# Feed-forward norms reach the features' partitions by block transposes and a way through DRAM instead of TensorE transposes

## The chip, the cores and the metric

The kernel runs on one core of a Trainium2 chip. The metric is the device time of one execution in microseconds (us). The engines are TensorE (PE in the profile; PEld is its weight load), VectorE (DVE), ScalarE (ACT), GpSimd (POOL) and SyncE (SP), which here only issues DMAs. All data is float32.

## The reference, cut to what matters

```python
# x: 4 sequences x 512 tokens x 256 features
n = layernorm(x)                                  # no gain, no bias
q = silu(n @ Wq1 @ Wq2);  f = sigmoid(n @ Wk1 @ Wk2);  v = n @ Wv
a = sigmoid(f)                                    # exp(log_sigmoid(f))
h = scan over tokens: h = a * h + (1 - a) * v
o = q * h;  o = o * rsqrt(mean(o * o) + 1e-6) * norm_w
x = x + layernorm(o @ Wo)

y = layernorm(x)
for i in range(6):
    y = gelu(y @ W1[i].T + B1[i]) @ W2[i].T + B2[i] + y     # 256 -> 1024 -> 256
    if i < 5:
        y = layernorm(y) * LN_G[i] + LN_B[i]
out = x + layernorm(y)
```

## The kernel before, in words

A tile holds 128 partitions. Matrix products want features on the partitions: an activation of one sequence is two tiles `xt` (128 features x 512 tokens). A norm wants tokens on the partitions, since its mean and variance run over the features: `sm` and `n` hold 128 tokens x 256 features. Going from one layout to the other is a transpose, done on TensorE by `transpose` (L504) into a PSUM tile and copied out by ScalarE (`to_features`).

The attention part runs first, over the 4 sequences. Then the feed-forward part runs over blocks i = 0 to 5 and, in each, over two groups g of two sequences (1024 tokens). For each (i, g):

- `Hidden` computes the first layer in 26 steps. Each step is two products of 256 columns (`product`, L493). The 4 x 2 by 2 x 4 blocks of the product are formed with fewer multiplications, from sums of weight blocks (`sa`, by `w1_sums`) and of blocks of the input (`tx`, by `input_sums`), both made by GpSimd (L459). The steps are in the text RESULT: the first is `a21 b10`, the second `s1 t1`, with t1 = b13 - b12. VectorE and ScalarE combine the products into the hidden blocks, and ScalarE applies the gelu (`Row.got`).
- `Row.got` also forms four sums t1 to t4 for the second layer, when all blocks of a row are there: t1 and t3 on VectorE (from `b12`, which lies in a PSUM bank), t2 and t4 on GpSimd. The blocks of row 0 come last, with the 26th step.
- `Output` computes the second layer with 28 products of 512 columns, four in each of the parts p1, p2, p6, p5, p7, p4, p3. The parts p4 and p3 are put off into the next `Hidden`. `partial` and `total` add bias and residual.
- `Norm` does the layer norm of that output while the next `Hidden` runs: `tokens` transposes it on TensorE (four 128x128 transposes per call, four calls), copies to `sm`, and takes statistics on VectorE; `rstd_of` gets the reciprocal deviation on GpSimd; `norm` normalizes on ScalarE into `n`; `features` transposes `n` back on TensorE (four transposes per call, four calls), and an activation applies gain and bias into `xt`. After the fourth, `input_sums` follows. In the last block there is no `features`: `norm` adds the attention's result x and stores. `Attended` has the same interface for the norm in front of block 0 (`ffn_input` also uses `to_features`).

The order of the work is not that of the source alone. `plan.op` records every operation with an engine, a cost, its reads and writes. `Plan.latest` gives each a due time, counted back from TensorE's sequence in the source; `Plan.run` simulates the engines with the costs, and at each moment lets an engine take the ready operation that is due first. The operations are issued in that order; every engine, and SP's queue of DMAs, then works in order on the chip. So a cost in the plan changes the order, not the operation. For DMAs the plan counts 0.3 us, the bytes, and 2.2 us.

Buffers are handed out by `Ring` (in turn) or `Pool` (taken and given back). `load` (L514) and `store` (L524) issue DMAs on SP: the inputs at the start, the 1 MB of `w1` and of `w2` for each block, and the outputs.

Of the kernel before, what the change touches and what calls it, by code (L numbers as in the profile page):

```python
# [16 lines left out]
P = 128  # L17
LN_EPS = 1e-5
SIGN = {"+": ALU.add, "-": ALU.subtract}
RMS_EPS = 1e-6  # L20
WARM = 6
# [52 lines left out]
p1 = s1 t1  # L74
# [95 lines left out]
class Ring:  # L170
# [5 lines left out]
    def next(self):  # L176
        buf = self.bufs[self.n % len(self.bufs)]
        self.n += 1
        if isinstance(buf, Grid):
            return buf.taken()  # L180
        buf.turn += 1
        return buf[:]


class Pool:


    def __init__(self, bufs):
        self.free = list(bufs)

    def next(self):
        buf = self.free.pop(0)
        buf.turn += 1
        return buf[:]

    def back(self, *views):
        self.free += [b for v in views for b in v.bufs]


class Grid:  # L200
# [9 lines left out]
    def taken(self):  # L210
        for b in sum(self.bufs, []):
            b.turn += 1
        lease = copy.copy(self)
        lease.views = {
            (m, k): self.view(m, k) for m in (None, 0, 1) for k in (None, 0, 1)
        }
        return lease
# [13 lines left out]
    def part(self, m=None, k=None):  # L231
        return self.views[m, k]


class Plan:
# [23 lines left out]
    def lag(self, before, after):  # L259

        a, b = self.ops[before], self.ops[after]
        if a[0] == b[0]:
            return 0.0
        return 0.35 if a[0] == "PE" else 0.2
# [64 lines left out]
def kernel(  # L329
# [41 lines left out]
    ps = ctx.enter_context(tc.tile_pool(name="ps", bufs=1, space=PSUM))  # L371
    ctx.enter_context(tc.manual_schedule())
# [12 lines left out]
    xs = [tiles(f"x{b}", [P, E], NT) for b in range(B)]  # L385
# [37 lines left out]
    hts = Ring([Grid(b.ap) for b in tiles("ht", [P, 2, S], NH)])  # L423
    tcs = Ring(tiles("tc", [P, S], 3 * NP))
    sms = Ring(tiles("sm", [P, 2, E], 4))
    nns = Ring(tiles("n", [P, E], 12))
# [8 lines left out]
    def act(dst, src, func=AF.Copy, bias=None, scale=None):  # L435
        given = [(k, p) for k, p in (("bias", bias), ("scale", scale)) if p is not None]
        ptrs = [p for _, p in given if isinstance(p, View)]
        kw = {k: p.ap if isinstance(p, View) else p for k, p in given}
        plan.op(
            "ACT",  # L440
            0.15 + 0.00083 * src.size + 0.11 * len(ptrs),
            lambda: nc.scalar.activation(dst.ap, src.ap, func, **kw)  # L442
            if func != AF.Copy
            else nc.scalar.copy(dst.ap, src.ap),  # L444
            [src, *ptrs],
            [dst],
        )
# [4 lines left out]
    def tt(engine, dst, a, b, alu):  # L452
        cost = 0.2 + 0.00209 * dst.size if engine == "POOL" else 0.06 + 0.00122 * dst.size
        if alu == ALU.pow:
            cost = 0.3 + 0.18 * dst.size
        plan.op(
            engine,
            cost,
            lambda: on(engine).tensor_tensor(dst.ap, a.ap, b.ap, alu),  # L459
            [a, b],  # L460
            [dst],
        )

    def tscalar(engine, dst, src, s0, s1, op0, op1=None):
        by = [s.ap if isinstance(s, View) else s for s in (s0, s1)]
        kw = {} if op1 is None else {"op1": op1}
        cost = (0.2 if engine == "POOL" else 0.15) + 0.0013 * dst.size
        if engine == "POOL":
            cost += 0.0017 * dst.size
        plan.op(  # L470
            engine,
            cost,
            lambda: on(engine).tensor_scalar(dst.ap, src.ap, *by, op0, **kw),  # L473
            [src, *(s for s in (s0, s1) if isinstance(s, View))],
            [dst],
        )

    def stt(dst, a, scalar, b, op0, op1):
        by = scalar.ap if isinstance(scalar, View) else scalar
        plan.op(  # L480
            "DVE",
            0.06 + 0.00133 * dst.size,
            lambda: nc.vector.scalar_tensor_tensor(dst.ap, a.ap, by, b.ap, op0, op1),  # L483
            [a, b, *([scalar] if isinstance(scalar, View) else [])],
            [dst],
        )
# [22 lines left out]
    def load(dst, src, engine="SP"):  # L509
        queue = nc.sync if engine == "SP" else nc.scalar  # L510
        plan.op(
            engine,
            0.45,
            lambda: queue.dma_start(out=dst.ap, in_=src),  # L514
            [],
            [dst],
            dst.size * P * 4 / 0.26e6,
        )

    def store(dst, src):  # L520
        plan.op(
            "SP",
            0.45,
            lambda: nc.sync.dma_start(out=dst, in_=src.ap),  # L524
            [src],
            [],
            src.size * P * 4 / 0.26e6,
        )
# [93 lines left out]
    def token_stats(mv, src, t):  # L622

        st = sts.next()

        def emit():
            nc.vector.bn_stats(st.ap, src.ap)  # L627
            nc.vector.bn_aggr(mv.ap[:, t, :], st.ap)  # L628

        plan.op("DVE", 0.59, emit, [src], [st, mv])  # L630
# [29 lines left out]
    def to_features(srcs, d, xt, scale=None, bias=None):  # L660
# [5 lines left out]
        if scale is None:  # L666
            act(xt, pt)
        else:
            act(xt, pt, AF.Identity, bias, scale)

    class Attention:
# [55 lines left out]
        def k1_q1(self):  # L727
            self.k1 = self.inner(wk1_s)
            self.q1 = self.inner(wq1_s)
            self.o, self.sq = [], []  # L730

        def value(self, e):
            self.psv = self.projected([wv_s[:, d, ts(e, P)] for d in range(ND)])

        def scan(self, e):
# [16 lines left out]
                1.3,  # L752
# [7 lines left out]
            o, sq = both.part(0), both.part(1)  # L760
            tt("POOL", o, q, h, ALU.mult)
# [23 lines left out]
        def residual(self):  # L785
# [4 lines left out]
            for t in range(NT):  # L790
                product(pss[:, t : t + 1], self.sq[-1][:, ts(t, P)], ones, True)
            ve = rs.next()[:, 0, :]
# [11 lines left out]
            for t in range(NT):  # L804
# [3 lines left out]
                token_stats(mv1, x1, t)  # L808
            self.x1_by = rstd_of(mv1, rs.next())
# [8 lines left out]
    class Row:  # L818
# [18 lines left out]
        def got(self, c, negative):  # L837
# [4 lines left out]
            if len(there) < 2:  # L842
                return
            if n == 1:
                self.b12 = banks.next()
# [11 lines left out]
            if len(self.there[1 - n]) == 2:  # L857
# [3 lines left out]
                tt("DVE", t1, self.b12, b11, ALU.subtract)  # L861
                tt("DVE", t3, b22, self.b12, ALU.subtract)
                banks.back(self.b12)
# [55 lines left out]
    class Output:  # L919


        def __init__(self, i, g, hidden):
# [5 lines left out]
            self.x = xts[g]  # L928
            self.a11 = [w[:, 2 * j, :P] for j in range(NP)]
            self.a12 = [w[:, 2 * j + 1, :P] for j in range(NP)]  # L930
            self.a22 = [w[:, 2 * j + 1, P:] for j in range(NP)]
            self.sf = [[None] * 2 for _ in range(ND)]
# [9 lines left out]

        def p1(self, j):
            if j == 0:
                self.px = banks.next()
            product(self.px, self.a11[j], self.hidden.rows[j].h[0][0], j == 0)
            if j == NP - 1:
                self.sn1 = self.partial(0, 0)

        def p2(self, j):  # L950
            if j == 0:
                self.py = banks.next()
            product(self.py, self.a12[j], self.hidden.rows[j].h[1][0], j == 0)
            if j == NP - 1:
# [3 lines left out]
        def p6(self, j):  # L958
            product(self.px, sb2[1][:, j, :], self.hidden.rows[j].sums[1], False)
            if j == NP - 1:  # L960
                self.sn2 = self.partial(0, 1)

        def p5(self, j):
            if j == 0:
                self.pz = [banks.next()[:, cols] for cols in self.parts]
            for pz, cols in zip(self.pz, self.parts):
                t1 = self.hidden.rows[j].sums[0]
                product(pz, sb2[0][:, j, :], t1[:, cols], j == 0)

        def p7(self, j):  # L970
            product(self.px, sb2[2][:, j, :], self.hidden.rows[j].sums[2], False)
            if j == NP - 1:
                self.s11 = self.partial(1, 1)
                if len(self.parts) == 1:
                    self.total11()

        def total11(self):
# [5 lines left out]
        def p4(self, j):  # L983
            product(self.px, self.a22[j], self.hidden.rows[j].sums[3], False)
            if j == NP - 1:
# [4 lines left out]
        def p3(self, j, part=0):  # L990
            pz, cols = self.pz[part], self.parts[part]
            b22 = self.hidden.rows[j].h[1][1]
            product(pz, sb2[3][:, j, :], b22[:, cols], False)
            if j == NP - 1:
# [9 lines left out]
    class Norm:  # L1004


        def __init__(self, i, g, output):
            self.i, self.g, self.output = i, g, output
            self.sm, self.by, self.n = [], [], []
# [25 lines left out]
        def norm(self, u):  # L1035

            for t in (2 * u, 2 * u + 1):
                z = normalized(self.sm[u][:, t % 2, :], self.by[t // NT], t % NT)
                self.n.append(z)
                if self.i == NB - 1:  # L1040
                    b, c = 2 * self.g + t // NT, t % NT
                    tt("POOL", z, z, xs[b][c], ALU.add)
                    store(out[b, ts(c, P), :], z)

# [14 lines left out]
        def features(self, u):  # L1059
            if self.i == NB - 1:  # L1060
                return
            n, d = divmod(u, ND)
            to_features(
                self.n[n * NT : (n + 1) * NT],
                d,
                xts[self.g][d][n],
                g_s[:, self.i, d : d + 1],
                be_s[:, self.i, d : d + 1],
            )
            if u == 2 * ND - 1:  # L1070
# [70 lines left out]
    for i in range(NB):  # L1141
        for g in range(NG):
            last, hidden = output, Hidden(i, g)
            hidden.take(2)
            if last:
                for j in range(NP):
                    last.p4(j)
            hidden.take()
            if last:
                last.p3(0)  # L1150
                last.p3(1)
            hidden.take()
            if last:
                last.p3(2)
                last.p3(3)
                norm = Norm(*of, last)
            if g == 0:
# [5 lines left out]
            for u in range(4):  # L1163
                hidden.take(2)
                norm.tokens(u)
            for u in range(4):
                hidden.take(2)
                norm.norm(u)
# [4 lines left out]
            for j in range(NP):  # L1173
                output.p1(j)
            for u, part in enumerate((output.p2, output.p6)):
                for j in range(NP):
                    part(j)
                    if j % 2:
                        norm.features(2 * u + j // 2)
            end = (i, g) == (NB - 1, NG - 1)  # L1180
            for j in range(NP // 2 if end else NP):
                output.p5(j)
            for j in range(NP):
                output.p7(j)
            of = (i, g)
    for j in range(NP // 2, NP):
        output.p5(j)
    output.total11()
    for j in range(NP):
        output.p4(j)  # L1190
    norm = Norm(*of, output)
    for part in range(2):
# [52 lines left out]
```

## Time and profile before

| what | value |
|---|---|
| median of 3 runs | 723.17 us (722.48 to 723.19) |
| the profiled execution's own time | 722.72 us |
| its span | 720.8 us |
| TensorE busy | 710.0 us, 98% |
| GpSimd busy | 500.3 us, 69% |
| VectorE busy | 419.4 us, 58% |
| ScalarE busy | 385.1 us, 53% |
| DMA | 19.18 MB |

All rows from the span on come from the one profiled execution. A busy share is an average over the whole span. TensorE's instructions overlap, so the length given for one record is longer than the pitch at which they follow each other; a product in float32 shows as two records. A line number in the profile is that of the helper that records the operation (L493 every product, L504 every transpose, L442 and L444 ScalarE's activations and copies, L459 every two-operand operation on VectorE or GpSimd), so groups are told apart by the names of their tiles.

### The profile page before, as it was taken

What the parts mean: (1) busy time and instruction counts of PE and PEld (TensorE: products, weight loads), DVE (VectorE), ACT (ScalarE), POOL (GpSimd) and SP (SyncE); (2) the same over time, 40 slices, a digit from 0 to 9 for tenths busy, and PEclk for the clock granted to TensorE, in tenths of its full rate; (3) what the DMA queues carried; (4) which work ended last, traced back from release to release, by engine and by line L of the source; (5) the groups of instructions that cost most, each with busy time, mean ns of one, the idle gap of its engine ahead of it and who ended that gap; (6) DMA issues with size and microseconds to landing.
All of it is one profiled execution on the core that took longest, in us unless ns stands there. A gap on an engine that the chain in (4) does not pass through costs nothing.

```text
span 720.8 us, 8269 instructions
## 1 busy us (share of the span) xinstructions
PE 710.0 (98%) x2712; PEld 474.8 (66%) x2712; DVE 419.4 (58%) x825; ACT 385.1 (53%) x669; POOL 500.3 (69%) x664
## 2 busy tenths in 40 slices
PE   9999999999999999999999999999999999999994
PEld 7565568658658568577576585684775765855853
DVE  5556556926728539449267286294492582772855
ACT  4757666726617527437357266274374472661732
POOL 4897768695874767963958856688639588466363
PEclk9999999999999999999999999999999999999997
DMA  7200010000110001010001100010100001000001
GB/s 243 95 1 1 0 39 20 2 1 0 59 58 1 0 1 60 0 59 1 1 0 60 58 1 1 0 25 35 60 0 1 0 1 29 31 1 0 30 25 63
DMA packets 14922, 19.18 MB, mean 27 GB/s; under 512 B 1568, under 2 KB 12832, under 8 KB 14880
## 3 DMA queue, kind: packets, MB, share of 16 engines
q1 hardware_dynamic: 14048, 17.74, 7.7%
q10 hardware_dynamic: 832, 0.92, 0.4%
q8 instruction: 21, 0.34, 0.2%
q14 instruction: 21, 0.17, 0.1%
HBM read 16.56 MB, written 2.10 MB: 26 GB/s over the span
## 4 chain that ended last, share of the span: by engine, by line
PE 97%; DMA 1%; DVE 1%; POOL 0%; ACT 0%; issue 0%; ACTq 0%; POOLq 0%
PE bank L493 87%; PE pt L504 6%; PE pt L493 4%; DMA xt<-in_wk 1%; DVE st L627 0%; DVE n L483 0%; POOL r L459 0%; ACT n L442 0%; POOL r L473 0%; DVE mv L628 0%; ACT L547 0%; DVE tmp L459 0%; ACTq L514 0%; POOLq L1241 0%; PE bank L504 0%
## 5 line engine op out<-in xcount | busy, mean ns | idle before, releaser
L444 ACT COPY tmp<-bank 128x512 f32<-128x512 f32 x144 | 84.1, 585 | 187.8 <-PE bank L493 175.2
L459 POOL TENSOR_TENSOR tc<-ht,tc 128x512 f32<-128x512 f32 x96 | 120.6, 1274 | 75.5 <-DVE st L627 43.7
L493 PE MATMUL bank<-tx,sa 128*128 128x256 f32 x672 | 161.2, 379 | 0.0
L493 PEld LDWEIGHTS bank<-tx,sa 128*128 128x128 f32 x672 | 125.1, 190 | 26.3 <-issue 8.6
L483 DVE SCALAR_TENSOR_TENSOR tmp<-bank,b,xt 128x512 f32<-128x512 f32 x48 | 36.0, 750 | 153.0 <-PE bank L493 153.0
L459 DVE TENSOR_TENSOR ht<-tmp,bank 128x512 f32<-128x512 f32 x156 | 101.1, 680 | 27.9 <-ACT tmp L444 24.3
L442 ACT ACTIVATE ht<-ht,b 128x512 f32<-128x512 f32 x144 | 99.4, 715 | 17.6 <-DVE ht L459 17.6
L493 PE MATMUL bank<-tc,w 128*128 128x512 f32 x208 | 95.0, 592 | 0.0
L493 PE MATMUL bank<-tc,sb 128*128 128x512 f32 (+1 forms) x200 | 90.0, 576 | 0.0
L493 PE MATMUL bank<-ht,sb 128*128 128x512 f32 (+1 forms) x200 | 88.3, 575 | 0.0
L493 PE MATMUL bank<-ht,w 128*128 128x512 f32 x192 | 86.2, 592 | 0.0
L459 DVE TENSOR_TENSOR tmp<-tmp,bank 128x512 f32<-128x512 f32 x96 | 64.8, 678 | 20.3 <-ACT tmp L444 9.9
L459 POOL TENSOR_TENSOR tx<-xt,tx 128x256 f32<-128x256 f32 x108 | 75.2, 728 | 1.0
L493 PEld LDWEIGHTS bank<-tc,w 128*128 128x128 f32 x208 | 39.1, 190 | 35.8 <-issue 33.2
L493 PEld LDWEIGHTS bank<-ht,sb 128*128 128x128 f32 x200 | 37.9, 190 | 35.0 <-issue 33.5
L493 PEld LDWEIGHTS bank<-ht,w 128*128 128x128 f32 x192 | 35.6, 190 | 35.5 <-issue 32.3
L442 ACT ACTIVATE n<-sm,r 128x256 f32<-128x256 f32 x104 | 54.1, 590 | 9.1 <-POOL r L459 9.1
L493 PE MATMUL bank<-tx,w 128*128 128x256 f32 x224 | 56.8, 379 | 0.0
L459 DVE TENSOR_TENSOR tmp<-bank,tmp 128x512 f32<-128x512 f32 (+1 forms) x54 | 35.9, 666 | 35.6 <-PE bank L493 33.9
L473 POOL TENSOR_SCALAR r<-mv 128x4 f32<-128x4 f32 (+1 forms) x72 | 20.7, 288 | 48.4 <-DVE mv L628 44.6
L442 ACT ACTIVATE xt<-pt,be,g 128x512 f32<-128x512 f32 x40 | 31.1, 777 | 38.8 <-PE pt L504 37.9
L493 PE MATMUL bank<-xt,sa 128*128 128x256 f32 x192 | 51.1, 379 | 0.0
(75 smaller groups left out, 1056.3 us busy)
## 6 DMA issues: line engine op xcount, KB each, us to landing
w<-in_w1t SPq DMA_DIRECT2D x6, 1024.0 KB, 5.1
w<-in_w2t SPq DMA_DIRECT2D x6, 1024.0 KB, 6.0
out<-n SPq DMA_DIRECT2D x16, 128.0 KB, 1.7
x<-in_x SPq DMA_DIRECT2D x14, 128.0 KB, 3.0
w<-in_wv ACTq DMA_DIRECT2D x1, 512.0 KB, 6.3
xt<-in_wo SPq DMA_DIRECT2D x4, 128.0 KB, 2.7
x<-in_x ACTq DMA_DIRECT2D x2, 128.0 KB, 3.0
w<-in_wk SPq DMA_DIRECT2D x1, 256.0 KB, 5.2
```

What stands on the lines that cost most here:

```text
L442: lambda: nc.scalar.activation(dst.ap, src.ap, func, **kw)
L444: else nc.scalar.copy(dst.ap, src.ap),
L459: lambda: on(engine).tensor_tensor(dst.ap, a.ap, b.ap, alu),
L473: lambda: on(engine).tensor_scalar(dst.ap, src.ap, *by, op0, **kw),
L483: lambda: nc.vector.scalar_tensor_tensor(dst.ap, a.ap, by, b.ap, op0, op1),
L493: lambda: nc.tensor.matmul(dst.ap, lhs.ap, rhs.ap, start=start, stop=True, skip_group_check=True),
L504: lambda: nc.tensor.transpose(dst.ap, src.ap, ident.ap),
```

## The change

- For blocks 0 to 4, `Norm.features` no longer transposes on TensorE. A new `passage` takes the four normalized tiles of a sequence. VectorE transposes them in blocks of 32x32 (two instructions of 128x512 elements), one store of 512 KB puts the result into a DRAM buffer, and eight loads of 64 KB bring it back with the 32-row strips on the right partitions, in runs of 128 elements. `features` is then one activation from SBUF to `xt`. A passage starts from the second call of `norm` for a sequence.
- The tiles of x serve as the buffers on both sides of the passage. So the attention's result is stored to DRAM (`kept`, 16 stores) and loaded again for the last block (`load_x`, 16 loads).
- `tokens` and `norm` now alternate by sequence (two calls of each, then two of each), and the parts of the second layer that are put off are spread over the first hidden steps.
- For row 0 (`POOLROWS`) the sums t1 and t3 move from VectorE to GpSimd, and `b12` stays in SBUF.
- The hidden and sum tiles (`ht`, `tc`) come from pools that are given back when their last product is recorded.
- The costs in the plan and its lags between engines get other values.

The diff, cut to its core:

```diff
+ORDER = "p1 p2 p6 p5 p7 p4 p3".split()
+DEFER = 8
+HEAD, BY = 2, (2, 1)
+POOLROWS = (0,)
...
     def lag(self, before, after):
-        if a[0] == b[0]:
-            return 0.0
-        return 0.35 if a[0] == "PE" else 0.2
+        if a[0] == "PE":
+            return 0.0 if b[0] == "PE" else 0.35
+        return {"DVE": 0.085, "ACT": 0.1, "POOL": 0.045}.get(a[0], 0.0) + 0.2 * (a[0] != b[0])
...
-            0.15 + 0.00083 * src.size + 0.11 * len(ptrs),
+            0.054 + 0.00084 * src.size + 0.11 * len(ptrs),
...
-        cost = 0.2 + 0.00209 * dst.size if engine == "POOL" else 0.06 + 0.00122 * dst.size
+        cost = 0.14 + 0.00213 * dst.size if engine == "POOL" else 0.07 + 0.00104 * dst.size
...
+    def passage(tokens):
+        block, there, to = blocked.next(), passed.next(), landed.next()
+        for k in range(0, NT, 2):
+            z0, z1 = tokens[k : k + 2]
+            pair = pairs[id(z0.bufs[0])].rearrange("p (t f r) -> p f t r", t=2, r=32)
+            dst = block.ap.rearrange("p (f t c) -> p f t c", t=NT, c=32)[:, :, k : k + 2, :]
+            plan.op("DVE", 0.6, lambda dst=dst, pair=pair: nc.vector.transpose(dst, pair),
+                [z0, z1], [block])
+        store(there, block)
+        src = there.ap.rearrange("(p r) (d q k) -> q r d p k", r=32, d=ND, q=Q)
+        dst = to.ap.rearrange("p (d g k) -> p d g k", d=ND, g=Q)
+        def emit():
+            for q in range(Q):
+                for d in range(ND):
+                    nc.sync.dma_start(out=dst[ts(q, 32), d], in_=src[q][:, d])
+        plan.op("SP", 0.45 * ND * Q, emit, [there], [to], to.size * P * 4 / 0.26e6)
+        blocked.back(block)
+        return to
...
             if n == 1:
-                self.b12 = banks.next()
+                self.b12 = self.h[0][1] if pool else banks.next()
...
-                tt("DVE", t1, self.b12, b11, ALU.subtract)
-                tt("DVE", t3, b22, self.b12, ALU.subtract)
+                tt("POOL" if pool else "DVE", t1, self.b12, b11, ALU.subtract)
+                tt("POOL" if pool else "DVE", t3, b22, self.b12, ALU.subtract)
...
+            if u % 2 and self.i < NB - 1:
+                n = u // 2
+                self.there[n] = passage(self.n[n * NT : (n + 1) * NT])
+
+        def load_x(self):
+            for b in (2 * self.g, 2 * self.g + 1):
+                for t in range(NT):
+                    xs[b][t] = xs[b][t].bufs[0][:]
+                    load(xs[b][t], kept[b][t])
...
     def features(self, u):
-            to_features(self.n[n * NT : (n + 1) * NT], d, xts[self.g][d][n],
-                g_s[:, self.i, d : d + 1], be_s[:, self.i, d : d + 1])
+            src, dst = self.there[n][:, ts(d, S)], xts[self.g][d][n]
+            act(dst.with_ap(dst.ap.rearrange("p (t g c) -> p g t c", t=NT, g=Q)),
+                src.with_ap(src.ap.rearrange("p (g t c) -> p g t c", t=NT, g=Q)),
+                AF.Identity, be_s[:, self.i, d : d + 1], g_s[:, self.i, d : d + 1])
...
-            hidden.take(2)
-            if last: (p4 four times)
-            hidden.take()
-            if last: (p3 twice)
-            hidden.take()
-            if last: (p3 twice)
+            if last:
+                hidden.take(HEAD)
+                while last.left:
+                    last.take(BY[0])
+                    hidden.take(BY[1])
...
-            for u in range(4):
-                hidden.take(2)
-                norm.tokens(u)
-            for u in range(4):
-                hidden.take(2)
-                norm.norm(u)
+            for us in ((0, 1), (2, 3)) if last else (range(4),):
+                for u in us:
+                    hidden.take(4//2)
+                    norm.tokens(u)
+                for u in us:
+                    hidden.take(4//2)
+                    norm.norm(u)
             hidden.take(26)
...
+            for u in range(4):
+                output.take(2 if u == 0 else 2)
+                norm.features(u)
+            output.take(len(output.left) - DEFER)
```

## The prediction

> **What bounds the kernel now.** I read the page first: busy shares, the slices, the chain that ended last.
>
> ```profile
> span 720.8 us, 8269 instructions
> PE 710.0 (98%) x2712; PEld 474.8 (66%) x2712; DVE 419.4 (58%) x825; ACT 385.1 (53%) x669; POOL 500.3 (69%) x664
> PEclk9999999999999999999999999999999999999997
> PE 97%; DMA 1%; DVE 1%; POOL 0%; ACT 0%; issue 0%; ACTq 0%; POOLq 0%
> ```
>
> TensorE is the chain: 97% of the span, at a full granted clock. A busy PE is not proof that it is at its peak, so I next read the windows of the feed-forward stage, one period for each block and token group, and the chain inside one of them.
>
> ```profile
> 173.30:223.30 50.00, 50.00 (x193) 33.40 (x192) 28.97 (x56) 26.20 (x44) 40.15 (x51) 1.00 0.13 42
> 223.30:273.30 50.00, 50.00 (x193) 33.41 (x192) 28.97 (x56) 26.21 (x44) 30.44 (x40) 1.00 0.00 1
> ...
> 190.50 0.44 PE pt L504 x4
> 190.94 1.72 PE bank L493 x4
> 192.66 0.44 PE pt L504 x4
> 193.10 2.58 PE bank L493 x6
> ```
>
> The columns of a window are length, busy PE, weight load, VectorE, ScalarE and GpSimd, then clock, DMA share and GB/s. Every period is 50.00 us with no gap. The code accounts for it: 26 steps of two 256-column products and 28 products of 512 columns, each step or product 0.862 us by the chain (x4 records take 1.72), is 54 x 0.862 = 46.55; plus 32 transposes, four in 0.434 us (the four start at 190.50, the next matmul at 190.94), is 3.47. Sum 50.02. So what TensorE issues is what a period costs, and half of the transposes are those of `features`, which the change removes.
>
> **The change, part by part.** The sum is made against the profiled execution: span 720.8 us, its own time 722.72, so 1.9 us lie around the span; the median of the runs shown, 723.17, is 0.45 above that.
>
> *PE transposes removed.* `Norm.features` ran for blocks 0 to 4 in both groups, four calls each of four transposes: 10 x 4 x 4 = 160, or 40 sets of 0.434 us: 17.4 us, all on the path. The Trainium skill, "VectorE: DVE Perf Modes", section "The three transpose paths", gives 390 ns for a 128x128 transpose on TensorE (for bf16). By it the same 160 would be worth 62 us; the trace's pitch of 0.109 us makes it 17.4. I take the trace: the row's 273 ns mean is one record's length, and records overlap.
>
> *VectorE.* 40 block transposes are added, each of 128x512 elements. No such row exists before. The nearest in shape is a tensor_tensor of 128x512:
>
> ```profile
> L459 DVE TENSOR_TENSOR tc<-bank,ht 128x512 f32<-128x512 f32 x48 | 32.3, 674 | 8.4 <-ACT bank L442 8.4
> L459 POOL TENSOR_TENSOR tc<-ht,tc 128x512 f32<-128x512 f32 x96 | 120.6, 1274 | 75.5 <-DVE st L627 43.7
> L442 ACT ACTIVATE xt<-pt,be,g 128x512 f32<-128x512 f32 x40 | 31.1, 777 | 38.8 <-PE pt L504 37.9
> ```
>
> I take 0.67 us: 27 us. The same section's 311 ns for a 128x128 set of blocks makes 1.24 us for four, 50 us in all; that is the upper bound, and 0.33 (half the row, one operand instead of two) the lower. `POOLROWS` takes two subtractions of row 0 away in 12 groups: 24 x 0.68 = -16 us. Net +11 us (bounds -3 to +34): VectorE at 416 to 453 of some 704 us, 64% at most. It stays under TensorE; nothing on the path.
>
> *ScalarE.* The 40 activations into `xt` stay at 0.78 us, from SBUF instead of PSUM; the row that reads and writes SBUF (`ht<-ht`, 0.715) says no worse. Cover: 26.2 busy of 50.
>
> *GpSimd.* The 24 subtractions come here at 1.27 us: 2.5 us per period. The heavier period goes from 40.15 of 50.0 to 42.7 of 48.3, 88%.
>
> *Queue and DMA.* SP gets 20 passages of one 512 KB store and eight 64 KB loads, 16 stores of x1 and 16 loads back: 212 issues of 0.33 to 0.43 us (the rows of `out` and `xt<-in_wo`), 70 to 91 us spread over the run. SP has that time:
>
> ```profile
> SPq L514 <- PE bank L493: 584.8, 10, 99.6
> ...
> w<-in_w1t SPq DMA_DIRECT2D x6, 1024.0 KB, 5.1
> w<-in_w2t SPq DMA_DIRECT2D x6, 1024.0 KB, 6.0
> out<-n SPq DMA_DIRECT2D x16, 128.0 KB, 1.7
> ```
>
> It mostly waits for TensorE to free a weight buffer. A passage's loads wait on its store, so a weight load behind them can start some 7 us late. `w1` is loaded one block early; `w2` lands at about 215 and TensorE first needs it at 235. A passage behind a weight load is not held long either: `w2_s` is free once `p4` has been issued, before step 6 of the next hidden layer, and the passages start after step 14. The x1 stores and the reloads have no reader within tens of us. All costed at nothing.
>
> *The wait that is added.* Before, four transposes and an activation led from a norm to `xt`. Now the way is transposes, store, loads, activation. TensorE no longer waits in `features`; it meets the result only at step 1 of the group's next hidden layer (`s1 t1`, t1 = b13 - b12, columns of the second sequence). The new order puts `tokens(3)` after step 18, so 8 steps, 20 products and one step lie between: 29 x 0.862 = 25.0 us. Against that, from the timeline of the period at 222.66, where the last token transposes end at 223.10: copy to `sm` +1.55 (to 224.65), statistics +1.6 (to 226.26), four GpSimd operations for the reciprocal deviation 1.93 (223.06 to 224.99), four normalizing activations 2.06, a block transpose 0.67, the store, the loads, two activations 1.5, one sum 0.73. For the store, between 128 KB in 1.7 and 1 MB in 5.1 us: 1.7 + 3.4 x 384/896 = 3.2. For eight loads: seven issues of 0.43 and one landing of 1.7 to 2.7 (rows of 128 KB): 4.7 to 5.7. The sum is 10.0 + 3.2 + 5.2 = 18.4 us. In-order engines can add one running instruction at each hand-over: 1.27 twice on GpSimd, 0.7 on ScalarE twice and once on VectorE, 4.6: 23.0. So 2.0 to 6.6 us are left, and I cost the wait at nothing. Lower bound: nothing too, since a wait cannot give TensorE time; upper: the first rival.
>
> A rule of the same section speaks against such a way: a plain DMA that transposes by strides is 19 times slower than the hardware's transpose when the innermost destination stride is large. Taken at its word, as an estimate on the 3.2 us of 512 KB, that is 61 us for a passage against a period of 50, and the change would be sunk. No run here shows such a transfer, and the rule's condition is not met: the strides lie outside, both ends run through 128 elements, 512 bytes, and VectorE turns the elements within the blocks. So I leave it out of the sum. The two weight rows bound the price of short runs: `w2`'s 1 KB rows take 0.9 us longer than `w1`'s 4 KB rows on 1024 against 256 of them, 1.2 ns for each; 1024 runs of 512 bytes cost a passage about 1.2 us more than the bytes, still under the time of the eight issues.
>
> *Order and durations in the plan.* They change who goes first. Before the change TensorE has no gap between 8.2 us and the tail, so there is nothing else to win except in the last 10 us, a chain through statistics and power that is left as it was. I allow -1 to +1.
>
> Sum: 720.8 - 17.4 = 703.4; + 1.9 = 705.3; + 0.45 = 705.8 at the median. I add 0.5 us for a few late hand-overs: 706.3.
>
> **The rivals.**
>
> *A: the passage is late, and TensorE waits at step 1 in ten periods.* Place: the first `t` sums of the next hidden layer. For it: the margin, and two DMA durations from no row of their own. Against it: the wait is known to the planner, whose figures are longer than mine together (its store 0.3 + 2.0 + 2.2 us, its loads the same), and which orders by due times. Price: each us beyond the margin costs up to 10. A half-late case, 0.3 to 1.5 us per period, gives 709 to 721. It decides for slower from 17.4 / 10 = 1.7 us per period: store and loads at 8.4 + 2.0 + 1.7 = 12.1 us if every hand-over waits, 16.7 if none does. At 3 us per period: 706 + 30 = 736.
>
> *B: GpSimd becomes the limit at row 0.* Row 0's last block comes with step 25, so its subtraction sits at the end of the hidden layer, with `p6` waiting for t2. Two operations of 1.27 instead of 0.67 + 1.27 make t2 later by 0.6 us; if the in-place t3 is put between them, by 1.9. For it: in the period at 173 GpSimd hardly rests from 188 to 211. Against: `p1` and `p2`, 6.9 us, come first, `p5` of the other rows can too, and the period at 223 has 20 us to spare. Half a us in each of 12 groups: 712.
>
> *C: the transposes' place is not free time.* The planner fills it, but something behind (a bank, a buffer taken later from the new pools) holds the same matmuls, and nothing is won: about 723. Against: one more bank is free at row 0, and evictions wait for TensorE (175.2 us on ScalarE, 153.0 on VectorE), not the reverse.
>
> **How the numbers follow.** Clean removal: 0.67 (704 to 708). B or a half-late A: 0.19 (708 to 721). C: 0.03. A beyond its deciding point, or an unseen cost of that size: 0.11. About 0.2%, 1.4 us, is what a measurement of this kernel can tell from no change. Faster 0.86, same 0.03, slower 0.11. The range 703.3 to 714.0 takes in the clean case with the tail's us, and the first half of B and A; above it lies some 0.17, below it 0.02.
>
> **What would show it.** Right: feed-forward periods of 48.3 us with a full PE; 160 fewer transposes on TensorE, none of `n` in blocks 0 to 4; 40 VectorE transposes near 0.67; store about 3.2, first issue to last landing of the loads about 5.2. Wrong: PE idle before matmuls on `tx` with GpSimd or ScalarE `xt` as releaser (A), before `tc,sb` with GpSimd as releaser (B), or before the first matmul into a bank (C); VectorE transposes over 1.3 us; loads that land 5 us after issue.

## The result and the profile after

The changed kernel takes 711.19 us (median of 4 runs, 710.47 to 711.97); the kernel before takes 722.92 us (722.48 to 723.19). The ratio is 0.9839, 95% interval 0.9821 to 0.9856: 11.7 us faster, where 16.9 had been forecast. The profiled execution took 711.97 us, with a span of 710.2. Of the experiments below, one execution each of `e1`, `e4` and `e5` took far longer (1273, 1541 and 818 us): it counts in their medians, which are 727.57, 728.09 and 712.87 us without it, but not in their ratios, and since it is the profiled one of `e4` and `e5`, no profile of these is used.

These rows of the changed kernel's page answer to those shown of before: span, busy time, granted clock, and shares of the chain that ended last.

```profile
span 710.2 us, 8330 instructions
...
PE 696.8 (98%) x2552; PEld 458.4 (65%) x2552; DVE 429.2 (60%) x841; ACT 382.3 (54%) x669; POOL 528.8 (74%) x688
...
PEclk9999999999999999999999999999999999999998
...
PE 87%; POOL 4%; DVE 2%; SPq 2%; ACT 2%; DMA 2%; issue 1%; ACTq 0%; POOLq 0%
```

TensorE has the 160 matmul records less, its busy time fell by 13.2 us, and its clock is still full. But its share of the chain fell from 97% to 87%: the end of the kernel now hangs on work of other engines in places where before it hung on TensorE alone. The windows of four feed-forward periods, each cut where a wait of TensorE ends, say where to look (columns as before):

```profile
176.10:224.64 48.54, 48.51 (x177) 31.86 (x177) 30.12 (x58) 26.31 (x45) 41.04 (x51) 1.00 0.28 87
224.64:273.13 48.49, 48.47 (x176) 31.83 (x176) 30.10 (x58) 25.95 (x45) 34.37 (x45) 1.00 0.14 44
273.13:322.60 49.47, 48.78 (x177) 31.78 (x177) 30.12 (x58) 26.19 (x45) 41.01 (x51) 1.00 0.28 85
322.60:371.09 48.49, 48.47 (x176) 31.84 (x176) 30.11 (x58) 25.96 (x45) 34.34 (x45) 1.00 0.14 44
```

Three periods are 48.5 us, 0.2 above the forecast 48.3, and one is 49.47. A busy sum hides the first of these: a matmul that starts late by 0.2 us leaves almost no hole in modelled ends. So I took the start times of all matmuls from the traces and summed what each start lies beyond the usual pitch of its width (0.431 us for 512 columns, 0.2155 for 256, 0.108 for 128; only excesses over 0.05 us). Worked out in this way, TensorE's lost time in us is:

```
stretch of the span (us)       before    after
8.5 to 104   attention           0.36     0.57
104 to 175   to the first norms  0.18     0.80
175 to 665   feed-forward        0.04     5.23
665 to end   last period, tail   0.41     1.85
```

After loses 7.5 us more than before in these. The first load comes 0.3 us later, and the time after the last matmul is 0.8 us shorter (9.55 to 8.79), which makes 7.0. It agrees with the two spans within 0.2: they differ by 10.6 us, 6.8 short of the 17.4 that the transposes were worth.

**The wait in every period (3.1 us over eleven).** Its places are 224.64, 273.13, 322.60 and so on, always at the step `p6 += s13 t8` of the hidden layer (p6 of RESULT, not the part p6 of the second layer). Three views of the timeline at the first of them, VectorE, ScalarE, then TensorE's weight load (start, length, engine, line, operation, tiles):

```profile
222.06 0.69 DVE L493 TENSOR_TENSOR ht<-tmp,bank 128x512 f32<-128x512 f32 x1
222.66 0.42 DVE L662 BATCH_NORM_STATS2 st<-sm 128x6 f32<-128x256 f32 x1
223.12 0.18 DVE L663 BATCH_NORM_AGGREGATE mv<-st 128x2 f32<-128x6 f32 x1
223.22 1.33 DVE L493 TENSOR_TENSOR tmp<-tmp,bank 128x512 f32<-128x512 f32 x2
```

```profile
222.78 0.59 ACT L478 COPY tmp<-bank 128x512 f32<-128x512 f32 x1 [0.38 <-DVE ht L493]
223.26 0.72 ACT L476 ACTIVATE ht<-ht,b 128x512 f32<-128x512 f32 x1
223.91 0.59 ACT L478 COPY tmp<-bank 128x512 f32<-128x512 f32 x1
```

```profile
221.64 2.56 PEld L525 LDWEIGHTS bank<-tx,sa 128*128 128x128 f32 x12
224.61 0.73 PEld L525 LDWEIGHTS bank<-tx,sa 128*128 128x128 f32 x4 [0.40 <-issue]
```

TensorE wants the PSUM bank that ScalarE's copy at 223.91 empties; the copy ends at 224.50, the weight load follows at 224.61 and the matmul at 224.64, 0.19 late. "issue" in the last row is only the profile's name for a wait that it could not place: the event before it is the end of that copy. The records do not name the bank, but the kernel's own sequence of operations, set beside them one by one, does: the copy reads the bank that the first VectorE operation of the 223.22 row reads, and it is the bank that `p6 += s13 t8` adds to. The copy starts 0.02 us after the signal that this read has ended (223.88), and the read had stood behind a token's statistics (222.66 and 223.12). ScalarE was not free much earlier: its activation of 223.26 runs up to the copy, late by the 0.38 us that the 222.78 copy had waited for VectorE's read of its bank in the 222.06 row.

**The late passage (2.0 us in two of ten periods).** SP's queue, then the chain of waits in the period at 273:

```profile
285.54 4.42 SPq L559 DMA_DIRECT2D passed<-x  x2
290.05 9.11 SPq L732 DMA_DIRECT2D x<-passed  x16
```

```profile
296.59 1.62 SPq L732
...
298.25 0.43 SPq L732
...
298.73 2.27 DMA x<-passed
...
301.02 0.82 ACT xt L476
...
301.91 0.74 POOL tx L493
...
302.69 1.35 PE bank L525 x5
```

In every period SP issues the stores of both sequences first, and then all 16 loads in a row, since its queue is in order. Here one issue lasted 1.62 us in place of 0.43. The last load landed at 300.99, 11.4 us after the last transpose had ended (289.60), and through `xt` and `tx` TensorE got its operand 0.83 us late at 302.69 (with the pitch of the matmul behind it, 0.93). At 400.75 it was 1.04 us, again from a landing at 11.4 (398.97, transposes ended at 387.55); there the last load took 3.49 us to land. In the period at 176, which is not late, the same way took 10.2 us (192.57 to 202.78). So a way of some 10.5 us (11.4 less the wait of 0.83 or 0.93) is still in time in these periods, the usual 10.2 leaves some 0.4 us of margin, and one slow DMA uses it up. What makes a DMA slow at times no run here shows.

**The tail (1.4 us).** At 692.64 the first p4 product of the last period waits until VectorE has read the bank that the p7 products filled, which p4 adds to:

```profile
692.64 3.67 PE L525 MATMUL bank<-tc,w 128*128 128x512 f32 x8 [0.94 <-DVE tmp L515]
```

### The profile page after: what moved, and what is told of

Its sections match the earlier page's. It is cut to its first block, busy times and chain, and to the rows that moved or that the text cites. A ratio compares the mean times of both kernels' runs of the same rounds, so it can differ in the third digit from the quotient of the medians.

```text
span 710.2 us, 8330 instructions
## 1 busy us (share of the span) xinstructions
PE 696.8 (98%) x2552; PEld 458.4 (65%) x2552; DVE 429.2 (60%) x841; ACT 382.3 (54%) x669; POOL 528.8 (74%) x688
## 4 chain that ended last, share of the span: by engine, by line
PE 87%; POOL 4%; DVE 2%; SPq 2%; ACT 2%; DMA 2%; issue 1%; ACTq 0%; POOLq 0%
PE bank L525 79%; PE pt L525 4%; PE pt L536 3%; SPq L732 2%; POOL r L493 1%; POOL sa L493 1%; POOL tc L493 1%; DVE ht L493 1%; DMA xt<-in_wk 1%; ACT n L476 1%; DMA x<-passed 1%; POOL r L505 0%; DVE st L662 0%; ACT ht L476 0%; ACT bank L476 0%
## 5 line engine op out<-in xcount | busy, mean ns | idle before, releaser
L525 PE MATMUL bank<-tx,sa 128*128 128x256 f32 x672 | 167.7, 381 | 1.8 <-POOL tx L493 1.4
L476 ACT ACTIVATE ht<-ht,b 128x512 f32<-128x512 f32 x156 | 107.1, 715 | 6.1 <-DVE ht L493 5.2
L525 PE MATMUL bank<-tc,sb 128*128 128x512 f32 (+1 forms) x200 | 85.0, 576 | 0.0
L525 PE MATMUL bank<-ht,w 128*128 128x512 f32 x192 | 84.7, 592 | 0.0
L505 POOL TENSOR_SCALAR r<-mv 128x4 f32<-128x4 f32 (+1 forms) x72 | 17.1, 237 | 88.7 <-DVE mv L663 85.1
L476 ACT ACTIVATE xt<-x,be,g 128x512 f32<-128x512 f32 x40 | 30.5, 807 | 68.9 <-DMA x<-passed 68.9
L525 PEld LDWEIGHTS bank<-tc,sb 128*128 128x128 f32 x200 | 37.6, 190 | 44.3 <-issue 30.8
L476 ACT ACTIVATE n<-sm,r 128x256 f32<-128x256 f32 x104 | 55.3, 594 | 11.4 <-POOL r L493 11.3
L478 ACT COPY sm<-pt 128x512 f32<-128x512 f32 (+1 forms) x60 | 31.7, 529 | 44.8 <-PE pt L536 28.9
```

Source lines behind the costliest of these rows:

```text
L525: lambda: nc.tensor.matmul(dst.ap, lhs.ap, rhs.ap, start=start, stop=True, skip_group_check=True),
```

## The experiments

The edits are against the changed kernel unless said; each kernel ran beside the kernel before, which took 722.95 to 723.30 us at the median.

**e1_pe_features.** The new order, pools, durations, row 0 on GpSimd and the way of x through DRAM stay; only the passage goes, and the features come back over TensorE as before.

```diff
     def features(self, u):
-            src, dst = self.there[n][:, ts(d, S)], xts[self.g][d][n]
-            act(dst..., src..., AF.Identity, ...)
+            to_features(self.n[n * NT : (n + 1) * NT], d, xts[self.g][d][n], ...)
     ...
-                self.there[n] = passage(self.n[n * NT : (n + 1) * NT])
```

> Undoes one part: the features of blocks 0 to 4 are again made by 160 TensorE transposes, with the new order, pools, durations, row 0 on GpSimd and the x tiles' way through DRAM kept. My theory: the transposes are worth their full 17.4 us, and what the changed kernel lacks to that is lost to small waits (about 3 us at one step of each period behind a ScalarE copy, 2 us where two passages are late, 1.4 us in the tail, 0.6 us at the hand-over from attention). The 2 us of late passages go away here, the other waits stay or fall as the order shifts: 711.2 + 17.4 - 2.0 = 726.6, slower than the kernel before. Rival 1 (the order and durations alone bring something): at or below 722. Rival 2 (the transposes were worth less than 17.4, since the freed time is lost again): below 724 with full periods of about 49 us instead of 50.

Measured: 727.61 us, ratio 1.0064 (1.0046 to 1.0082). The transposes are worth 16.4 us (727.61 - 711.19), near the 17.4 of the sum; the rest of the change costs 4.6 us. The wait of each period is not the passage's: without any passage it stands in all eleven periods, 2.94 us for the ten of them that lie between 175 and 665. It is this row among the waits of `e1`, with total, times and longest:

```profile
PEld bank L525 <- ACT tmp L478: 4.7, 11, 0.4
```

**e2_old_durations.** The costs and lags in the plan are those of before.

```diff
-            return 0.0 if b[0] == "PE" else 0.35
-        return {"DVE": 0.085, "ACT": 0.1, "POOL": 0.045}.get(a[0], 0.0) + 0.2 * (a[0] != b[0])
+        return 0.0 if a[0] == b[0] else 0.35 if a[0] == "PE" else 0.2
     ...
-            0.054 + 0.00084 * src.size + 0.11 * len(ptrs),
+            0.15 + 0.00083 * src.size + 0.11 * len(ptrs),
     (and six more costs)
```

> The changed kernel with the plan's old costs and lags; all operations the same, only their order differs. My theory: the refitted costs are a little too tight, so that the ScalarE copy before the second half of p6 comes 0.2 us late in every period; old, larger costs keep it in time and the periods go from 48.5 to 48.3 us: 708 to 709. Rival: the old costs make the planner give the passages and row 0's sums wrong ranks, TensorE waits before the second layer's products on banks or on sums, and the time is over 713, up to that of the kernel before; then the refit is a needed part of the change and not a loss.

Measured: 729.6 us, 1.009 (1.0071 to 1.0108). My theory fell: the passage gains nothing at all with the old figures. With them the plan lets ScalarE do the eight normalizing activations of a group in one block, ahead of the gelus. The four block transposes of these tiles then stand close together on VectorE (240.03 to 243.76), among the sums of the second layer, and TensorE waits there (ScalarE's timeline, then TensorE's):

```profile
238.09 4.04 ACT L475 ACTIVATE n<-sm,r 128x256 f32<-128x256 f32 x8 [0.38 <-POOL r L492]
```

```profile
244.40 0.44 PE L537 MATMUL pt<-ident,tmp 128*128 128x128 f32 x2 [1.31 <-DVE tmp L492]
```

**e3_no_row_on_gpsimd.** The sums t1 and t3 of row 0 go back to VectorE, `b12` to a bank.

```diff
-POOLROWS = (0,)
+POOLROWS = ()
```

> POOLROWS empty: t1 and t3 of row 0 are back on VectorE, b12 back in a PSUM bank; all else as changed. My theory: the tail's stall of 1.1 us (p4 waiting for VectorE to have read the bank after p7) comes from row 0's sums being late, which made TensorE take its filling work early; without it the tail gets 1 us back and the rest is the same: about 710. Rival: the bank that the move frees is what the second layer needs now that no transposes lie between its parts; without it TensorE waits about 1 us per group for a bank before its first products of the second layer: 711.2 + 10 to 13 = 721 to 724.

Measured: 726.66 us, 1.0053 (1.0035 to 1.0071). My theory fell here as well, and the rival had the size but not the cause. No free bank is lacking. The chain at the end of a hidden layer lies on VectorE without a break:

```profile
240.26 0.58 DVE tc L493
240.84 1.53 DVE ht L493
242.36 0.60 DVE tc L493
242.96 0.59 DVE ht L493
243.56 0.67 DVE tmp L515
244.23 0.14 issue
244.37 2.81 PE bank L525 x6
```

Block transposes (three between 237.2 and 240.2), the sums of row 0 and the partial result of the second layer meet there, and TensorE waits until the partial result has been read out of the bank that it adds to next: 1.76 us in each of the five lighter periods between 175 and 665. In the heavier ones it waits 0.89 us for a sum on GpSimd. An engine that is some 60% busy over the span is full in this stretch.

**e4_before_new_durations.** The kernel before, with the new costs and lags alone.

> The kernel before with the new costs and lags of the plan alone. My theory: it has no gap in its feed-forward periods and can win nothing there; with tighter costs it may lose up to 0.3 us per period: 722.9 to 725. Rival: the refit by itself is worth 1 us or more in head and tail: under 722.

Measured: 728.39 us, 1.0073 (1.0055 to 1.0091). The fitted figures make the old kernel 5.3 us slower, near the 4.6 that `e1` lost.

**e5_four_loads.** Four loads of 128 KB for a passage in place of eight of 64 KB; the plan's cost for the issues is halved.

```diff
             for q in range(Q):
-                for d in range(ND):
-                    nc.sync.dma_start(out=dst[ts(q, 32), d], in_=src[q][:, d])
+                nc.sync.dma_start(out=dst[ts(q, 32)], in_=src[q])
```

> The changed kernel, but a passage comes back in four loads of 128 KB (both feature halves in one) instead of eight of 64 KB; the plan's cost of the step halves with them. My theory: in the periods at 302 and 400 us the second passage came late because SP issued sixteen loads in a row at 0.47 us each; with eight it lands 3 to 4 us earlier, the two waits of TensorE before its first product on tx (0.9 and 1.0 us) go away: 711.2 - 2.0 = 709.2, and the spread of the runs gets smaller. Rival: the loads' landing, not their issue, made it late (one DMA took 3.5 us instead of 2.1); larger loads land later by as much: 711.

Measured: 713.0 us, 0.9855 (0.984 to 0.9871), where 709.2 was expected: no gain, but 1.8 us more than the changed kernel. Why is told under `e10`.

**e6_bank_reads_in_plan.** The copy's rows above led to this one. In the plan, a read depended on the writer of its buffer alone, so two engines could read one bank in any order or at once. In the program on the chip the copy starts only after VectorE's read has ended. The edit tells the plan so; no operation is added or taken away.

```diff
         for b in (b for v in reads for b in v.bufs):
             deps.add(b.writer)
+            if b.psum:
+                deps.update(b.readers)
     ...
+    for b in [*banks.free, *pts.bufs]:
+        b.bufs[0].psum = True
```

> The changed kernel, but the plan counts a read of a PSUM bank by one engine as a dependency of the next read of that bank by another; no operation changes, only the order. In the traces ScalarE's copy of such a bank starts 0.02 us after VectorE's read of it has ended, and the plan knows nothing of that. My theory: this is why TensorE finds the copy before the second half of p6 late in each period; with the dependency in the plan the 0.29 us go away in ten or eleven periods: 711.2 - 3.0 = 708.2. Rival: the copy is late because the costs are too small in general; the order changes, but a wait of the same size comes back elsewhere: 710 to 712.

Measured: 706.13 us, 0.9764 (0.9751 to 0.9778): 5.1 us below the changed kernel, more than I had expected. Lost time between 175 and 665 fell from 5.23 to 1.18 us. The wait of each period is gone, and the hand-over between attention and feed-forward (0.6 us at 143.7 and 144.2 in the changed kernel) with it. The two late passages are gone too, because they begin earlier: in the period at 273 the last transpose ends at 287.19, 14.3 us after `p6 += s13 t8` at 272.89, where it was 16.5 (289.60 - 273.13). What is left are waits before `tc,sb` products, for GpSimd, in every second period, and 0.9 us of the tail.

**e7_four_loads_bank_reads.** Both edits.

> Four loads and bank reads in the plan together. My theory: both losses are independent and add: 711.2 - 2.0 - 3.0 = 706.2, and what is left to the 705.8 of the sum is the tail. Rival: they share a cause or trade with each other: 708 or more.

Measured: 704.62 us (704.16 to 704.72), 0.9741 (0.9727 to 0.9755). It is the best version, 6.6 us below the changed kernel, and beats both. Its page and two of its periods:

```profile
span 702.8 us, 8211 instructions
...
PE 692.4 (99%) x2552; PEld 459.8 (65%) x2552; DVE 427.4 (61%) x841; ACT 380.2 (54%) x669; POOL 529.2 (75%) x688
...
PE 97%; DMA 1%; POOL 1%; DVE 0%; ACT 0%; issue 0%; ACTq 0%; POOLq 0%
```

```profile
226.50:274.74 48.24, 48.24 (x178) 31.98 (x177) 29.79 (x58) 24.63 (x43) 34.52 (x47) 1.00 0.14 45
274.74:323.05 48.31, 48.31 (x178) 31.89 (x177) 30.22 (x58) 27.13 (x47) 40.95 (x50) 1.00 0.28 87
```

This is the picture that the prediction drew: TensorE is 97% of the chain again, and its periods are 48.3 us with no gap.

**e8_before_new_durations_bank_reads.** The edit of `e6` on the kernel of `e4`.

> The kernel before with the new costs (which alone made it 728.4) and with bank reads as dependencies in the plan. My theory: the old, larger costs of the plan covered the unplanned order of bank reads; the new ones don't, and that is the 5.3 us: with the dependency known, 723 to 724. Rival: the new costs are too small in other places: 727 or more.

Measured: 723.96 us, 1.001 (1.0002 to 1.0018). Of the 5.3 us that the fitted figures cost before (a ratio of 1.0073), 0.7 is left. That the old, larger figures had left more room around the reads is likely, but not shown. The order alone costs nothing: in the kernel before, 32 of the 144 copies start 0.033 to 0.035 us after VectorE's read of their bank, and no wait of TensorE comes of it.

**e9_pe_features_bank_reads.** The edit of `e6` on the kernel of `e1`.

> As the kernel with bank reads in the plan (706.1), but the features of blocks 0 to 4 made by 160 TensorE transposes again. My theory: with the small waits gone, nothing but TensorE's own work separates the two, so the difference is the 17.4 us of the sum: 706.1 + 17.4 = 723.5 less the 0.5 us of waits beside the passages: 723.0, the time of the kernel before; so the other parts of the change bring nothing by themselves. Rival: order and pools are worth something by themselves: under 721.

Measured: 722.48 us, 0.9993 (0.9985 to 1.0002). Against `e6` this is the passage alone, in a plan that keeps the reads apart: 722.48 - 706.13 = 16.35 us, and 17.9 us against `e7`. The order, the pools, the move of row 0 and the durations bring nothing without the passage.

**e10_four_loads_again.** The kernel of `e5` once more, for a profile.

> The kernel with four loads alone once more, for an undisturbed profile (its 713.0 was 1.8 us more than the changed kernel, where I had expected 2.0 less). My theory now: the passages are in time there (no wait at about 302 and 400 us), but the plan, which took the loads' cost down too, orders ScalarE and VectorE differently and the wait behind the bank copies grows: PE gaps of over 0.3 us in each period at a place with ScalarE's copy as releaser. Rival: the late passages are still there, and the larger loads land later.

One execution: 711.95 us, span 709.8. The late passages are gone, as expected: no gap is left near 302 or 400, and the way takes 7.9 to 10.0 us where it took 9.9 to 11.4. But the bank's wait, with the pitch behind it, has grown from 0.28 to 0.36 us in most periods, and new ones of 0.4 us stand before `tc,sb` in every second one, ended by a VectorE operation. Between 175 and 665 it loses 5.8 us, more than the changed kernel. So four loads do mend the queue, and the gain is lost to other small waits; with the bank reads in the plan (`e7`) it is kept.

**e11_best_no_row_on_gpsimd** and **e12_best_old_durations.** The edits of `e3` and of `e2`, now on the best version.

> Four loads and bank reads in the plan, but t1 and t3 of row 0 on VectorE and b12 in a bank. My theory: VectorE is dense at the end of a hidden layer, the block transposes lie there, and without the move TensorE waits at p6 in each period, as in the run without it before (15.5 us over the changed kernel): 704.6 + 12 to 16 = 717 to 720. Rival: that wait came from the plan's ignorance of bank reads; with them known it is under 708.

> Four loads and bank reads in the plan, but the old costs and lags. My theory: the old costs overrate VectorE and ScalarE by 0.1 us or so per instruction, so that work due later is put off into the end of the hidden layer, and TensorE waits there whether the bank reads are known or not: 715 to 728. Rival: the refit was only dangerous or useful because of the bank reads; with them known the old costs do as well: 704 to 707.

Measured: 718.6 us, 0.9939 (0.9922 to 0.9956), 14.0 above the best, and 719.88 us, 0.996 (0.9945 to 0.9975), 15.3 above it. Both parts are needed also when the bank reads are planned. In `e11` TensorE waits for the partial result again, 1.49 and 0.80 us in turn from period to period. In `e12` it waits for VectorE in every period (1.05 and 0.58 us in turn, with the pitch behind) and for a sum of GpSimd in every second one (0.73). These are its waits for the two (total, times, longest):

```profile
PE bank L530 <- DVE ht L496: 6.5, 10, 0.9
...
PE bank L530 <- POOL tc L496: 2.9, 5, 0.6
```

## Why the prediction was right, and what was mis-sized

- **TensorE is the bound, and the 160 transposes are worth 17.4 us.** Right. `e1` against after gives 16.4, `e9` against `e6` 16.35, `e9` against `e7` 17.9. Between two waits a period is clean: 273.13 - 224.64 = 48.49, less the 0.27 us of waiting that lies in it, is 48.22.
- **"Late hand-overs", 0.5 us.** This is the term that was mis-sized. With the tail and the start, it was 6.8 us against the spans. I had put it in as a small allowance with no row behind it. The runs show the plan's ignorance of the order of two engines' reads of one bank to be behind most of it: the edit that mends only this gives 5.1 us here, 4.4 on the kernel of `e4`, and 5.1 on that of `e1`. Rival C (a bank or a buffer that holds the same matmuls) was nearest to it, but I had priced it as all or nothing, at 723; a bank that holds two matmuls in each period for 0.3 us was not among the cases. That 711.2 still lies in the range is in part luck: the room up to 714 was left for half of A and B, of which A came to 2.0 us and B to nothing, and it was filled by a cost that had no part in the sum.
- **The passage.** The pieces were near. These rows answer to the values taken (the page, and the groups by form for the first; of a DMA row the last number is from issue to landing):

```profile
L721 DVE STREAM_TRANSPOSE x<-n 128x512 f32<-128x512 f32 x40 | 28.0, 700 | 1.3 <-ACT n L476 1.3
```

```profile
L476 ACT ACTIVATE xt<-x,be,g 128x512 f32<-128x512 f32 x40 | 30.5, 807 | 68.9 <-DMA x<-passed 68.9
...
passed<-x SPq DMA_DIRECT2D x20, 512.0 KB, 2.8
x<-passed SPq DMA_DIRECT2D x160, 64.0 KB, 2.1
```

  A block transpose takes 0.70 us (0.67 taken), the store 2.8 (3.2), the loads of a passage 5.3 from first issue to last landing (5.2): in the period at 176 the store is issued at 192.60 and lands at 195.41, the loads are issued from 197.45 and the last lands at 202.78. Of the factor of 19 that the prediction took from the Trainium skill ("VectorE: DVE Perf Modes", section "The three transpose paths") and left out, since its condition is not met, nothing is seen: its estimate was 61 us for a passage. What I had missed is that two passages share one queue: between the store's landing and the first load lie 2.0 us, in which SP issues the other sequence's loads. So the way is 10.2 us long against the 8.4 of the sum, and the margin, worked out as 2.0 to 6.6 us, is 0.4. TensorE's stretch was right: in the period at 273 from the end of the last token transposes (276.7) to where `s1 t1` would have started (301.86) are 25.2 us, 25.0 in the sum. But from there to the end of the last block transposes (289.60) are 12.9 us, where the sum had 7.8 without and 12.4 with every hand-over. On GpSimd alone the four operations of the reciprocal deviation went from 282.48 to 286.74, 4.3 us in place of 1.93, because sums of weights lie between them. "The wait costs nothing" was wrong by 2.0 us, in two periods of ten: a small rival A.
- **"VectorE stays under TensorE; nothing on the path."** True of the kernel as it is, but argued from a share of 64%, which could not show it. `e3` and `e11` lose 15.5 and 14.0 us when 16 us of sums go back to VectorE. In the same way "order and durations" were taken as worth -1 to +1; without the fitted figures 15 to 18 us are lost (`e12`, `e2`).
- **GpSimd** was right: 41.0 of 48.5 us in the heavier period (42.7 of 48.3 forecast), and rival B did not come in the changed kernel. GpSimd's sums end the small waits before `tc,sb` in `e6`, and some of those in `e3` and `e12`.
- **The tail**, -1 to +1, came out at +1.4 in waits and -0.8 after the last matmul, so inside its bounds.

Open: in the changed kernel's trace 3.1 us stand as waits for a bank and 2.0 as late passages, and the edit of `e6`, which changes the order of all engines' work, took away both. Why VectorE's transposes come 2.2 us earlier in its order was not tried by itself.

## What to carry to other kernels

When work is taken off the engine that bounds a kernel, the forecast of what is freed is the easy part; look next for what stands a few tenths of a us behind that engine in every period, in start times rather than in busy sums. A planner must know every order that the chip's program keeps, here that of two reads of one bank, and here finer costs made an order that it did not know of dearer, not cheaper. Judge a helper engine by the densest stretch in which it has new work, not by its share of the span.

## What the runs showed of the hardware that was not expected

- **Two readers of one PSUM bank go one after the other.** In the changed kernel 21 of 144 copies `tmp<-bank` start 0.034 to 0.035 us after the end of a VectorE operation that reads the same bank and shares no other buffer with the copy. With the banks told by the kernel's sequence of operations, no read of a bank by ScalarE overlaps one by VectorE, in the traces of before, of after and of `e6`. The Trainium skill, "PSUM — Partial Sum Buffer", section "PSUM bank collisions raise a hardware error", says that any two engines on one bank (in the same 32 partitions) at once collide, two reads included, and that the program has to order them. The trace agrees with the order; no run here shows a collision.
- **A VectorE operation with two SBUF inputs waits for a GpSimd sum beside it.** The row of `ht<-tmp,tmp` (groups by form) of before, then of `e11`:

```profile
L459 DVE TENSOR_TENSOR ht<-tmp,tmp 128x512 f32<-128x512 f32 x12 | 8.2, 685 | 0.0
```

```profile
L497 DVE TENSOR_TENSOR ht<-tmp,tmp 128x512 f32<-128x512 f32 x12 | 14.2, 1187 | 0.0
```

  VectorE's and GpSimd's timelines of `e11` at one of the long ones:

```profile
241.32 1.62 DVE L497 TENSOR_TENSOR ht<-tmp,tmp 128x512 f32<-128x512 f32 x1
```

```profile
238.55 5.53 POOL L497 TENSOR_TENSOR tc<-ht,tc 128x512 f32<-128x512 f32 x4 [1.09 <-DVE tc L497]
```

  GpSimd's third sum had begun 0.19 us before, and VectorE's took 1.62 us in place of 0.69. Where GpSimd's began 0.95 us before, VectorE's took 0.87. The rule in the traces is plain: wherever a sum of GpSimd had more than 0.2 us left when this operation began (28 places in after, `e7` and `e11`), the operation ended 0.54 to 0.55 us after that sum. The 1.53 us of `ht` in the chain of `e3` is the same operation; by an estimate from the lengths, 0.9 of the 1.5 us that TensorE waits in a lighter period of `e11` come from it. The Trainium skill, "SBUF — State Buffer", section "Who interferes with whom", says that a VectorE instruction with two SBUF inputs and a GpSimd instruction that reads SBUF shut each other out, and that the one issued first goes first; these lengths agree. The block transposes, with one input, stayed at 0.69 to 0.70 us.
- **A wait of TensorE costs a little more than its length.** After most waits the next start comes 0.29 to 0.32 us later in place of 0.216 (302.69, then 303.01), so 0.19 us of waiting cost 0.27 to 0.29.
